# Second convolution of a residual block: two of six column positions also filtered along rows, norm sums of three images on ScalarE, and a map of two chunks between the convolutions

## The chip, the cores and the metric

The kernel runs on one core of a Trainium2 chip. The metric is the device time of one execution in microseconds; the page of the profile describes one profiled execution, and its "span" runs from that execution's first to its last instruction. The engines are named TensorE (PE; its weight loads are PEld), VectorE (DVE), ScalarE (ACT), GpSimd (POOL) and SyncE (SP). SP issues plain transfers, POOL issues those that add to their destination. A convolution of the code is written as matmuls in fp32, and each of them is two instructions in the trace.

## What is computed

Four layers on x of 4 images, 256 channels and 56 x 56 pixels. Every layer adds to x a function of its group norm. Layers 0 and 2 are involutions, layer 3 is a gating by means; only layer 1, a residual block of two 3 x 3 convolutions, is touched by the change:

```python
def _L1_conv_ref(x, w1, g1, b1, rm1, rv1, w2, g2, b2, rm2, rv2):
    h = _conv3x3(x, w1, stride=1)
    h = _bn(h, g1, b1, rm1, rv1)
    h = jax.nn.relu(h)
    h = _conv3x3(h, w2, stride=1)
    h = _bn(h, g2, b2, rm2, rv2)
    return jax.nn.relu(x + h)
...
def _gn(v, G=32, eps=1e-5):
    g = v.reshape(B_, G, C_ // G, H_, W_)
    m = jnp.mean(g, axis=(2, 3, 4), keepdims=True)
    s = jnp.var(g, axis=(2, 3, 4), keepdims=True)
    return ((g - m) / jnp.sqrt(s + eps)).reshape(v.shape)
...
x = x + _L1_conv_ref(_gn(x), L1_conv_w1, ...)
x = x + _L2_conv_ref(_gn(x), L2_conv_w1, ...)
```

The group norm of layer 2 needs a mean and a variance per channel of what layer 1 puts out.

## The kernel before

**Chunks.** An image goes through both convolutions in three chunks of rows: C1_ROWS (L56) for the first, C2_ROWS (L57: 16, 20 and 20 rows) for the second; with four images there are twelve chunks of each. The 256 channels are two halves (NB = 2) of 128 partitions. A list `order` alternates them: first convolution of chunk i, second convolution of chunk i - 1, and so on, with two chunks of the second convolution at the end.

**Columns.** Along a row, both convolutions work on transformed data: four output columns come from six products, the column positions k, with KS = (1, 2, 3, 4, 0, 5) as their order. `phases` (L1363, ScalarE at L1379) norms the loaded rows and spreads them into `ph1` by the column modulo 4; `transform` (L1382 to L1425, nine steps of VectorE) makes the six planes of a tile `v` from that. Two rows of each plane are kept from the chunk before (L1386).

**Rows.** The second convolution takes each position as it is: `unfiltered` (L1478 to L1484) sums six matmuls, three row taps times two input halves, for each output half, 12 per position, each over 14 columns times all rows of the chunk (280 columns at 20 rows, 224 at 16). The first convolution does better from its second chunk on: its positions are *filtered* along rows, two output rows from four products in place of six. `columns` (L1443) makes the inputs: an "inner" pair (sum and difference of two neighbouring rows, VectorE, L1464 and L1465) and an "outer" pair (difference of rows two apart: a multiplication by -1 on ScalarE, L1457, and a transfer from POOL that adds the other row, L1458). Then 16 matmuls of half the rows follow (L1520; 126 columns at 18 rows, 140 at 20). ScalarE copies the first product out of PSUM (L1529), VectorE forms difference and sum with the second (L1533, L1534) and adds the outer pair (L1536). The weights for this are formed once (`column_weights`, three VectorE instructions L1316 to L1318, and `filter_weights`, L1309).

**After the products.** In the second convolution VectorE and ScalarE join the positions (L1643 to L1666), position 0 and 5 by output half. `joined` then takes a half out: ScalarE scales it into a residual tile x (L1603), a transfer from POOL adds the input (L1604), ScalarE takes the relu (L1606), a second transfer adds the input again (L1607), and SP stores it (L1608). `late_r` puts the last three behind slots of the chunk that follows. In the chunk after that, VectorE takes the sums for the next norm from x with bn_stats (`stats`, L1633). The two last chunks take another way, with a residual tile `res` that both halves share (L1578, L1587, L1611, L1616).

**Order.** Every engine's order is that of the program (`in_order`). A chunk has twelve slots, `after[0]` to `after[11]`, two for each position, and the step loop (L1717 to L1801) drops other work into them: the transforms of the next chunks, the columns, the sums. So an instruction placed in a slot stands in its engine's queue between those of two positions.

**PSUM.** The stage has a pool of four tiles of two banks (L1187). An unfiltered position takes one, a filtered one two.

```python
            KS = (1, 2, 3, 4, 0, 5)

            def filtered(i):

                return KS[: (0, 5, 6)[min(i, 2)]]
...
                    place(after, late_v, (0, 0, 0, 1, 1))
...
                        place(after, input1(j), (1, 1, 2, 2, 3, 3, 4, 4, 5))
```

Of the kernel before, what the change touches and what calls it, by code (L numbers as in the profile page):

```python
# [16 lines left out]
P = 128  # L17
# [38 lines left out]
C1_ROWS = [(0, 20), (20, 38), (38, 56)]  # L56
# [16 lines left out]
def net_kernel(  # L73
# [1109 lines left out]
    def conv_layer(xin, xout, st, ahead):  # L1183
        with ExitStack() as es:
# [51 lines left out]
            v2_sb = wpool.tile([P, 2 * NY], F32, name="v2_sb")  # L1236

            def new_v2(half):

                n_v2[half] += 1  # L1240
                at = (n_v2[half] - 1) % 4
                if half:
                    return [room["v2"][:, at * NY : (at + 1) * NY]]
                if at == 3:
                    return [room[r][:, 5 * NY : 5 * NY + NY // 2] for r in ("v2", "xr")]
                t = room["v2"][:, 4 * NY : 5 * NY] if at == 2 else v2_sb[:, at * NY : (at + 1) * NY]
                return [t[:, : NY // 2], t[:, NY // 2 :]]
# [63 lines left out]
            def column_weights(ci, k0, k1):  # L1311

                w0, w1, w2 = (u1_sb[:, ci, y, k0:k1, :] for y in range(3))
                x = between_weights(ci, k0, k1)
                s = y_tile(5 if k0 == 5 else 3)[:, : (k1 - k0) * C].rearrange("p (k n) -> p k n", n=C)
                tt(s, w0, w2, ALU.add)  # L1316
                tt(x, s, w1, ALU.subtract)
                tt(w1, s, w1, ALU.add)  # L1318


            PL, VP = (0, 2, 1, 3), (0, 1, 2, 3, 5, 4)
            ph1 = wpool.tile([P, 4, CV_ROWS + 2, NB, WT + 1], F32, name="ph1")
            ph2 = wpool.tile([P, 4, H + 2, NB, WT + 1], F32, name="ph2")
# [3 lines left out]
            for j in range(4):  # L1327
                for y in (0, H + 1):
                    nc.gpsimd.memset(ph2[:, j, y], 0.0)
# [33 lines left out]
            def phases(i):  # L1363

                y0, y1, lo, hi = rows1(i)
                n, r0, known = y1 - y0 + 2, lo - (y0 - 1), 2 if i % 3 else 0
# [5 lines left out]
                for ci in range(NB):  # L1372
                    at = ci * (CV_ROWS + 2) * W
                    xr = room["rows"][:, at + known * W : at + (hi - lo) * W].rearrange("p (r t j) -> p j r t", t=WT, j=4)
                    for j in range(4):
                        q, t0 = (j + 1) % 4, (j + 1) // 4
                        dst = ph1[:, PL[q], r0 + known : r0 + hi - lo, ci, t0 : t0 + WT]
# [4 lines left out]
            def transform(v, ph, y0, n, known):  # L1382

                if known is not None:
                    old, m = known
                    nc.scalar.copy(  # L1386
                        v[:, :, : 2 * NB].rearrange("p k r t -> p k (r t)"),
                        old[:, :, m * NB : (m + 2) * NB].rearrange("p k r t -> p k (r t)"),
                    )
                    v, y0, n = v[:, :, 2 * NB :], y0 + 2, n - 2  # L1390
# [36 lines left out]
            v_sb = [wpool.tile([P, WPOS, (CV_ROWS + 2) * NB, WT], F32, name=f"v{k}") for k in range(2)]  # L1427

            def input1(i):
                y0, y1, _, _ = rows1(i)  # L1430
                v = v_of[1, i] = v_sb[min(i, 1)]
                p0, p1 = C1_ROWS[i % 3 - 1]
                known = (v_of[1, i - 1], p1 - p0) if i % 3 else None
                yield from transform(v, ph1, 0, y1 - y0 + 2, known)

            def input2(i):
                y0, y1 = C2_ROWS[i % 3]
                v = v_of[2, i] = v_sb[i == n_chunks - 1]
                p0, p1 = C2_ROWS[i % 3 - 1]
                known = (v_of[2, i - 1], p1 - p0) if i % 3 else None  # L1440
                yield from transform(v, ph2, y0, y1 - y0 + 2, known)

            def columns(i, k, half):  # L1443

                y0, y1, _, _ = rows1(i)
                n = y1 - y0
                m = n // 2
                v = v_of[1, i][:, VP[k]]
                if half:
                    (t,) = new_v2(1)  # L1450
                    v = v.rearrange("p r t -> p (r t)")
                    at = slice(0, n * NB * WT)
                    below = slice(2 * NB * WT, (n + 2) * NB * WT)
                    if i == 1:
                        tt(t[:, at], v[:, at], v[:, below], ALU.subtract)
                    else:
                        nc.scalar.mul(t[:, at], v[:, below], -1.0)  # L1457
                        nc.gpsimd.dma_start(t[:, at], v[:, at], accum_op=ALU.add)  # L1458
                    t = t.rearrange("p (r e n) -> p e r n", e=2, n=NB * WT)
                    v2_of[i, k, 1] = [t[:, e] for e in range(2)]  # L1460
                else:
                    v = v.rearrange("p (r e c) t -> p e r (c t)", e=2, c=NB)
                    t = v2_of[i, k, 0] = [x.rearrange("p (r n) -> p r n", n=NB * WT) for x in new_v2(0)]
                    tt(t[0][:, :m], v[:, 1, :m], v[:, 0, 1 : m + 1], ALU.add)  # L1464
                    tt(t[1][:, :m], v[:, 0, 1 : m + 1], v[:, 1, :m], ALU.subtract)  # L1465


            FIRST = [(k, half) for k in KS[:4] for half in range(2)]
# [16 lines left out]

            def conv1(i, after, tail):
# [3 lines left out]
                m = n // 2 * WT  # L1490
                a, t, b, s, q = (y_tile(k)[:, : NB * n * WT] for k in (0, 1, 2, 5, 4))
                first = s if i else q
                home = {1: s, 2: q, 3: t, 4: s, 0: y_tile(3)[:, : NB * n * WT], 5: s}

                def outputs(*js):
                    for j in js:
                        o = (a, t, b, q)[j].rearrange("p (c r t) -> p c r t", c=NB, t=WT)
                        p, t0 = PL[(j + 1) % 4], (j + 1) // 4
                        for co in range(NB):
                            nc.scalar.activation(  # L1500
                                ph2[:, p, y0 + 1 : y1 + 1, co, t0 : t0 + WT],
# [7 lines left out]
                for n_s, k in enumerate(KS):  # L1509
                    if k in filtered(i):  # L1510
                        va = v2_of[i, k, 0]
                        vb = v2_of[i, k, 1]
# [372 lines left out]
```

## Time and profile before

| what | us |
|---|---|
| median of 3 runs (range) | 1740.52 (1738.83 to 1744.15) |
| the profiled execution | 1735.74 |
| its span | 1733.9 |
| stage of the two convolutions | about 518 to 1186 |
| in that stage: PE, DVE, ACT, POOL busy | 662, 553, 295, 117 |

The stage's first matmul of a convolution starts at 517.87 us and its last ends at about 1186. Before and behind it are layer 0 and layers 2 and 3, in which the code is the same but for the place of their buffers. Busy time of an engine is the sum over its instructions; "idle before" is the time the engine waited, put down to what ended it. TensorE's clock was granted at 1.00 in every window of this stage that is shown.

### The profile page before, as it was taken

Reading aid. Unit: us, or ns where it says so; the run is one execution under the profiler, and the core shown is the slowest. Engines: PE = TensorE matmul, PEld = TensorE weight load, DVE = VectorE, ACT = ScalarE, POOL = GpSimd, SP = SyncE. Lnnn points to the kernel's source line nnn. Section 1 sums busy time; section 2 is a strip of 40 time slices with the busy share of each in tenths; the row PEclk is TensorE's granted clock in tenths of the full one; section 3 lists DMA queues with packets and bytes.
Section 4 is the critical chain, followed back from the end, with each engine's and each line's share of the span. In section 5 each row is a group of like instructions: output and inputs, shape, how many; then the busy total and the mean of one; then the engine's idle time right before and its main releaser. Section 6 shows DMA issues by size and latency. Waiting matters only on the chain.

```text
span 1733.9 us, 56359 instructions
## 1 busy us (share of the span) xinstructions
PE 1664.7 (96%) x24296; PEld 1479.3 (85%) x24296; DVE 1317.1 (76%) x2467; ACT 933.5 (54%) x2024; POOL 476.4 (27%) x669
## 2 busy tenths in 40 slices
PE   6999999999999999999999999998999899999998
PEld 4998998888977999898899889986988788788886
DVE  2777787777769887798878888856787678778775
ACT  2655556456646455443455245325667567577564
POOL 2223322323334111211122111100000563563571
PEclk9999999999989999999999999999999999999996
DMA  2455444543659546454565354553444666664652
GB/s 89 129 167 162 137 151 160 166 129 103 220 184 260 95 106 142 76 125 96 119 143 97 82 118 92 100 167 104 147 142 151 206 208 196 210 209 161 203 161 103
DMA packets 89030, 252.15 MB, mean 145 GB/s; under 512 B 14453, under 2 KB 35966, under 8 KB 85070
## 3 DMA queue, kind: packets, MB, share of 16 engines
q1 hardware_dynamic: 57438, 163.33, 29.1%
q0 software_dynamic: 30304, 83.95, 22.6%
q8 instruction: 192, 3.15, 0.8%
q10 hardware_dynamic: 1040, 1.26, 0.3%
q14 instruction: 56, 0.46, 0.1%
HBM read 95.07 MB, written 49.15 MB: 83 GB/s over the span
## 4 chain that ended last, share of the span: by engine, by line
PE 70%; DVE 15%; DMA 4%; ACT 4%; issue 3%; SPq 2%; POOL 2%; ACTq 0%; POOLq 0%; DVEq 0%
PE mm L1482 22%; PE ps L593 14%; PE ps L635 14%; PE mm L1520 11%; DVE kt L611 5%; PE ps L407 3%; DVE un L655 3%; DMA xw<-xw 2%; DMA u_sb<-in_wc_dram 2%; PE ps L469 2%; DVE st L1105 1%; ACT hp L488 1%; SPq L425 1%; ACT kt L604 1%; PE ps L718 1%
## 5 line engine op out<-in xcount | busy, mean ns | idle before, releaser
L1482 PE MATMUL mm<-v,u_sb 128*128 128x280 f32 (+2 forms) x1896 | 422.8, 384 | 0.7 <-DVE xs L1534 0.7
L1482 PEld LDWEIGHTS mm<-v,u_sb 128*128 128x128 f32 x1896 | 357.8, 189 | 62.2 <-issue 1.7
L635 PE MATMUL ps<-kt,xw 126*32 126x48 f32 (+1 forms) x12544 | 378.9, 235 | 20.9 <-issue 8.2
L635 PEld LDWEIGHTS ps<-kt,xw 126*32 126x32 f32 (+1 forms) x12544 | 340.6, 121 | 65.8 <-issue 41.5
L593 PE MATMUL ps<-hp,z_sb 64*126 64x133 f32 x6144 | 385.2, 279 | 9.2 <-DVE kt L611 5.0
L593 PEld LDWEIGHTS ps<-hp,z_sb 64*126 64x126 f32 x6144 | 365.1, 186 | 25.7 <-DVE kt L611 7.1
L611 DVE TENSOR_TENSOR kt<-ps,zb_sb 126x798 f32<-126x798 f32 x352 | 333.0, 980 | 59.4 <-PE ps L593 59.0
L604 ACT ACTIVATE kt<-ps,zb_sb 126x133 f32<-126x133 f32 x960 | 281.0, 442 | 108.4 <-PE ps L593 108.4
L655 DVE SCALAR_TENSOR_TENSOR un<-ps,s,un 128x240 f32<-128x240 f32 x224 | 102.4, 457 | 83.4 <-ACT un L650 79.3
L1520 PE MATMUL mm<-xs,u_sb 128*128 128x126 f32 (+1 forms) x1296 | 159.7, 277 | 4.4 <-DVE xs L1534 2.6
L655 DVE SCALAR_TENSOR_TENSOR un<-ps,par_sb,un 128x240 f32<-128x240 f32 x224 | 97.5, 456 | 82.0 <-ACT un L648 78.1
L1520 PEld LDWEIGHTS mm<-xs,u_sb 128*128 128x128 f32 x1296 | 153.3, 191 | 5.4 <-issue 2.9
L660 POOL TENSOR_TENSOR xs<-un,xs 128x240 f32<-128x240 f32 x112 | 72.1, 665 | 216.1 <-DVE un L655 216.1
L419 ACT COPY xw<-ps 126x896 f32<-126x896 f32 x112 | 101.4, 906 | 41.7 <-DMA xw<-xw 22.8
L1458 POOL DMA_DIRECT2D xs<-v x60 | 52.8, 1015 | 249.4 <-ACT xs L1457 248.5
L407 PE MATMUL ps<-ident_sb,strip_sb 128*126 128x128 f32 x784 | 111.6, 282 | 7.7 <-issue 4.3
L150 POOL TENSOR_TENSOR norm_sb<-norm_sb,mhalf 128x1 f32<-128x1 f32 x32 | 19.2, 601 | 360.5 <-DVE norm_sb L149 360.5
L648 ACT ACTIVATE un<-ps,par_sb 128x240 f32<-128x240 f32 x112 | 50.3, 449 | 119.4 <-PE ps L635 109.8
L650 ACT ACTIVATE un<-ps,bn_t,s 128x240 f32<-128x240 f32 x112 | 60.2, 538 | 88.2 <-PE ps L635 80.0
L407 PEld LDWEIGHTS ps<-ident_sb,strip_sb 128*126 128x126 f32 x784 | 84.2, 140 | 19.5 <-issue 5.4
L1603 ACT ACTIVATE xs<-hp,raw,raw 128x1120 f32<-128x1120 f32 (+1 forms) x20 | 45.2, 2260 | 97.7 <-DVE hp L1666 97.7
L1379 ACT ACTIVATE ph<-xs,norm_sb 128x294 f32<-128x294 f32 (+2 forms) x96 | 80.7, 865 | 9.5 <-DMA xs<-x 7.6
(291 smaller groups left out, 2010.0 us busy)
## 6 DMA issues: line engine op xcount, KB each, us to landing
xw<-xw SPq DMA_DIRECT2D x224, 252.0 KB
xw<-xw SPq DMA_DIRECT2D x224, 126.0 KB
xs<-x POOLq DMA_DIRECT2D x26, 560.0 KB, 5.9
x<-xs POOLq DMA_DIRECT2D x8, 1568.0 KB, 8.2
xs<-x SPq DMA_DIRECT2D x8, 1568.0 KB
xs<-v POOLq DMA_DIRECT2D x42, 252.0 KB, 4.2
xs<-in_x_dram SPq DMA_DIRECT2D x6, 1568.0 KB
x<-xs SPq DMA_DIRECT2D x6, 1568.0 KB
```

The source lines that it names most:

```text
L407: nc.tensor.transpose(ps[:Q, k * P : (k + 1) * P], flat[:, k * Q : (k + 1) * Q], ident_sb)
L419: nc.scalar.copy(xw[:, :NSB, :], ps[:Q, : NSB * P].rearrange("q (n c) -> q n c", n=NSB))
L593: nc.tensor.matmul(ps[:Q, i, k * NT : (k + 1) * NT], z_sb[i * R : (i + 1) * R, cb * GB // 2 + gp, z0 : z0 + Q], hp[i * R : (i + 1) * R, py ...
L604: nc.scalar.activation(kt[:, g0 + i, pb, :, k], ps[:Q, i, k * NT : (k + 1) * NT], AF.Identity, bias=zb_sb[:, cb * GB + g0 + i, p0 + k : p0 ...
L611: nc.vector.tensor_tensor(kt[:, g0 : g0 + 2, pb], ps[:Q, :, : PB * NT].rearrange("q i (k t) -> q i t k", k=PB), zb_sb[:, cb * GB + g0 : cb ...
L635: nc.tensor.matmul(v[m * j : m * j + m, i, :, k * TP : (k + 1) * TP], xw[:, window(ty), m * j : m * j + m], kt[:, ng * j : ng * j + ng, :, ...
L650: nc.scalar.activation(part, o[0], AF.Identity, bias=bn["t4"][:, cb : cb + 1], scale=bn["s4"][ng][:, 0, cb : cb + 1])
L655: nc.vector.scalar_tensor_tensor(part, o[e], s, part, ALU.mult, ALU.add)
L660: nc.gpsimd.tensor_tensor(dst, u, dst, ALU.add)
L1379: nc.scalar.activation(dst, xr[:, j], AF.Identity, bias=t, scale=s)
L1482: nc.tensor.matmul(ps, *position(u, v, ci, dy, k, co, n), start=(j == 0), stop=(j == NB * 3 - 1))
L1520: nc.tensor.matmul(ps[:, bank, co * m : (co + 1) * m], u[ci][:, co * P : (co + 1) * P], v2[e][:, : n // 2, ci * WT : (ci + 1) * WT], start ...
```

## The change

- *Two positions of the second convolution* (FILTERED2 = (4, 0)) are filtered along rows in every chunk, in the way of the first convolution. `filtered_product` is now shared. New weights (`column_weights2`, `filter_weights2`) are formed in the first chunk of the second convolution.
- *Inputs.* `inner_columns` takes two positions in one instruction; the pair (1, 2) goes into planes of `ph1` that are free then, so `phases` of the next chunk moves to later slots. `outer_columns` shares five buffers among both convolutions. The pair (0, 5) of the first convolution is made in its slot 0, its outer rows in slots 0 and 2.
- *Position 0* of the second convolution is now joined for both halves at once; position 5 stays by half. The two last chunks have a residual tile for each half.
- *Norm sums.* For images 0 to 2 bn_stats on VectorE goes. ScalarE runs over x twice with its accumulator: once for the mean, once, squared with the mean as bias, for the spread. Image 3 keeps bn_stats.
- *The way out.* The second half's first step (`leaves`) stands behind slot 0 of the next chunk; the store moves from slot 9 + 2 co to 11 + 2 co; the passes for the sums come at 10 + 2 co and 14 + 2 co (slots of 12 and more lie in the chunk after).
- *Rows and map.* C1_ROWS is 18, 20, 18, and `ph2`, which held a whole image between the convolutions, holds two chunks of 20 rows in turn, with an edge row set to zero where one is needed. The transform of the second convolution's chunk takes 19, 20 and 19 new rows (18, 20 and 20 before), and one of its steps moves from the second convolution's slot 0 to the first convolution's slot 10.

```diff
-C1_ROWS = [(0, 20), (20, 38), (38, 56)]
+C1_ROWS = [(0, 18), (18, 38), (38, 56)]
+PH_ROWS = 20
...
+            def new_inner(ks):
+                if ks == (1, 2):
+                    t = ph1[:, 1::2].rearrange("p k r c t -> p k (r c t)")[:, :, :NY]
+                else:
+                    n_v2[0] += 1
+                    t = v2_sb[:, n_v2[0] % 2]
...
+            FILTERED2 = (4, 0)
+            def column_weights2(ci, k):
+                s = y_tile(5)[:, :C]
+                column_sums_of(*(u2_sb[:, ci, y, k, :] for y in range(3)), ux2_sb[FILTERED2.index(k)][:, ci], s)
...
-            ph2 = wpool.tile([P, 4, H + 2, NB, WT + 1], F32, name="ph2")
+            ph2 = wpool.tile([P, 4, 2 * PH_ROWS, NB, WT + 1], F32, name="ph2")
...
+            def inner_columns(conv, i, *ks):
...
+                tt(t[:, :, 0, :m], v[:, :, 1, :m], v[:, :, 0, 1 : m + 1], ALU.add)
+                tt(t[:, :, 1, :m], v[:, :, 0, 1 : m + 1], v[:, :, 1, :m], ALU.subtract)
...
+            def outer_columns(conv, i, k):
...
+                if (conv, i) == (1, 1):
+                    tt(t[:, at], v[:, at], v[:, below], ALU.subtract)
+                else:
+                    nc.scalar.mul(t[:, at], v[:, below], -1.0)
+                    nc.gpsimd.dma_start(t[:, at], v[:, at], accum_op=ALU.add)
...
+            def filtered_product(conv, i, k, home, weights, between, items):
...
+                inner, outer = two_banks(), two_banks()
+                work4 = ((inner, 0, va[0], u1), (inner, 1, va[1], between), (outer, 0, vb[0], u0), (outer, 1, vb[1], u2))
+                for ps, bank, v2, u in work4:
+                    for co in range(NB):
+                        for ci in range(NB):
+                            nc.tensor.matmul(
+                                ps[:, bank, co * m : (co + 1) * m],
+                                u[ci][:, co * P : (co + 1) * P],
+                                v2[:, : n // 2, ci * WT : (ci + 1) * WT],
+                                start=(ci == 0),
+                                stop=(ci == NB - 1),
+                            )
...
+                nc.scalar.copy(o[:, 0], m1)
+                tt(o[:, 1], o[:, 0], m2, ALU.subtract)
+                tt(o[:, 0], o[:, 0], m2, ALU.add)
+                run_all(items)
+                tt(o, o, outer[:, :, : NB * m].rearrange("p e (r t) -> p e r t", t=WT), ALU.add)
...
+                        def leaves():
+                            nc.scalar.activation(x.rearrange("p (q j) -> p j q", j=4), y, AF.Identity, bias=t, scale=s)
+                            nc.gpsimd.dma_start(x, xin[bb][co][:, at], accum_op=ALU.add)
+                        if co == 0:
+                            leaves()
+                        else:
+                            late_r[0].append(leaves)
+                        k = 5 + 2 * co
                         late_r[k].append(lambda: nc.scalar.activation(x, x, AF.Relu, scale=by))
                         late_r[k + 1].append(lambda: nc.gpsimd.dma_start(x, xin[bb][co][:, at], accum_op=ALU.add))
-                        late_r[k + 4].append(lambda: nc.sync.dma_start(xout[bb][co][:, at], x))
+                        k = 10 + 2 * co
+                        late_r[k + 1].append(lambda: nc.sync.dma_start(xout[bb][co][:, at], x))
+                        if bb < B - 1:
+                            st = sums[co][:, i % 3]
+                            late_r[k].append(lambda: mean_of(st, x))
+                            late_r[k + 4].append(lambda: spread_of(st, x))
...
+                def mean_of(st, x):
+                    nc.gpsimd.memset(st[:, 0:1], float(n * W))
+                    nc.scalar.activation(x, x, AF.Identity, accum_out=st[:, 1:2])
+                    nc.scalar.mul(st[:, 1:2], st[:, 1:2], 1.0 / (n * W))
+                def spread_of(st, x):
+                    c = small.tile([P, 1], F32, name="c")
+                    nc.scalar.mul(c, st[:, 1:2], -1.0)
+                    nc.scalar.activation(x, x, AF.Square, bias=c, accum_out=st[:, 2:3])
...
-                for n_s, k in enumerate(KS[:4]):
+                for n_s, k in enumerate(KS[:5]):
+                    if n_s == 4:
+                        residual(0)
+                    if k in filtered2(i):
+                        ux = [ux2_sb[FILTERED2.index(k)][:, ci] for ci in range(NB)]
+                        filtered_product(2, i, k, s, u2_sb, ux, after[2 * n_s])
...
+                    else:
+                        stt(full(p), full(p), -0.75, got, ALU.mult, ALU.add)
+                        stt(p, r, 0.25, p, ALU.mult, ALU.add)
...
-                    ps = one_bank()[:, :m]
-                    unfiltered(ps, u2_sb, v, 0, co, n)
-                    stt(p[:, at], p[:, at], -0.75, ps, ALU.mult, ALU.add)
-                    stt(p[:, at], r[:, at], 0.25, p[:, at], ALU.mult, ALU.add)
...
-                tail += [[lambda co=co, k=k: stats(co, k) for k in range(ST_PIECES[i % 3])] for co in range(NB)]
+                if not summed or bb == B - 1:
+                    tail += [[lambda co=co, k=k: stats(co, k) for k in range(ST_PIECES[i % 3])] for co in range(NB)]
...
-                        place(after, late_v, (1, 3, 5, 8))
+                        place(after, late_v, (1, 3, 5, 8, 10))
...
-                            place(after, phases(i + 1), range(1, 10))
+                            place(after, phases(i + 1), range(4, 12))
...
-                        place(after, late_v, (0, 0, 0, 1, 1))
+                        place(after, late_v, (0, 0, 1, 1))
...
+                    if filtered2(i):
+                        after[2].append(lambda i=i: inner_columns(2, i, *filtered2(i)))
+                        for n, k in enumerate(filtered2(i)):
+                            after[2 + n].append(lambda i=i, k=k: outer_columns(2, i, k))
...
-                        for n, (k, half) in enumerate(FIRST):
-                            after[(5, 5, 6, 6, 7, 7, 8, 8)[n]].append(lambda j=j, k=k, half=half: columns(j, k, half))
+                        columns_at(after, (6, 8), ((4, 1), (4, 2), (6, 3), (9, 4)), 1, j)
```

## The prediction

> **What bounds the kernel now.** I read the page first: TensorE is busy nearly all the time, which alone says little. Columns: busy us, share of the span, instructions.
>
> ```profile
> span 1733.9 us, 56359 instructions
> PE 1664.7 (96%) x24296; PEld 1479.3 (85%) x24296; DVE 1317.1 (76%) x2467; ACT 933.5 (54%) x2024; POOL 476.4 (27%) x669
> ```
>
> Only the middle stage, about 518 to 1186 us, is touched, so the chain of waits there came second. Columns: start, us, what.
>
> ```profile
> 575.49 5.10 PE mm L1482 x24
> ...
> 663.45 22.88 PE mm L1520 x192
> ...
> 849.67 33.96 PE mm L1482 x144
> 883.63 21.44 PE mm L1520 x192
> 905.07 27.25 PE mm L1482 x144
> ```
>
> The reader is to see one engine without gaps: a second-convolution chunk (L1482) follows a first-convolution chunk (L1520) to the tenth of a microsecond. From 608 to 1183 us this chain is almost all TensorE, so here TensorE time removed is time won, unless another engine closes up. These rows price a matmul (each matmul of the code is two instructions in the trace): 33.96/144 = 235.8 ns at 280 columns, 27.25/144 = 189.2 at 224, 5.10/24 = 212.5 at 252, 22.88/192 = 119.2 at 140, 21.44/192 = 111.7 at 126.
>
> Third, windows by chunk, for what VectorE and ScalarE have left. Columns: window, length, then busy time of PE, PEld, DVE, ACT, POOL, the granted clock, DMA share and GB/s.
>
> ```profile
> 580.57:607.90 27.33, 27.33 (x148) 27.31 (x147) 24.30 (x43) 8.73 (x17) 4.61 (x6) 1.00 0.22 38
> 607.90:629.40 21.50, 21.50 (x194) 21.50 (x193) 17.79 (x36) 16.73 (x27) 5.09 (x6) 1.00 0.77 145
> 849.50:883.50 34.00, 34.00 (x147) 27.26 (x146) 27.88 (x51) 8.39 (x12) 4.40 (x5) 1.00 0.35 90
> 883.50:904.90 21.40, 21.40 (x193) 21.40 (x192) 17.54 (x35) 15.79 (x24) 4.36 (x5) 1.00 0.82 150
> 904.90:932.10 27.20, 27.20 (x146) 27.18 (x145) 25.32 (x45) 7.60 (x12) 3.53 (x4) 1.00 0.41 109
> 954.30:988.40 34.10, 34.09 (x146) 27.36 (x146) 28.63 (x49) 7.34 (x10) 4.37 (x5) 1.00 0.29 66
> ```
>
> VectorE is 82 to 93% busy, ScalarE under a third in the second convolution and three quarters in the first. VectorE is the engine that can close up. Its prices, from the groups of instructions by shape (count, then busy us and mean ns):
>
> ```profile
> L1633 DVE BATCH_NORM_STATS2 st<-xs 128x6 f32<-128x448 f32 x36 | 22.3, 619 | 0.0
> L1536 DVE TENSOR_TENSOR xs<-xs,mm 128x560 f32<-128x560 f32 x9 | 6.6, 737 | 2.3 <-PE mm L1520 1.7
> L1534 DVE TENSOR_TENSOR hp<-hp,mm 128x280 f32<-128x280 f32 x9 | 4.0, 447 | 0.3
> L1606 ACT ACTIVATE xs<-xs,norm_sb 128x1120 f32<-128x1120 f32 x12 | 14.7, 1224 | 0.0
> ```
>
> [...]
>
> **The change part by part.**
>
> *Filtered positions, 20-row chunks (8 of them).* Position by position, 24 instructions of 235.8 ns (5.66 us) become 32 of 140 columns, 119.2 ns (3.81). 1.85 x 2 positions x 8 chunks = -29.6 us, all on the path.
>
> *16-row chunks (4).* 24 x 189.2 = 4.54 us become 32 of 112 columns. No row shows 112. [...] the 126-column row a floor of 111.7. I take the floor[...]: 32 x 0.1117 = 3.57, saving 0.97 x 2 x 4 = -7.7 us. [...]
>
> *VectorE per 20-row chunk of the second convolution.* Added: inner sums of two positions, 2 x 0.74; the products' combination, 2 x (2 x 0.45 + 0.74) = 3.3. Removed: six bn_stats of the chunk before, 4 x 0.62 + 2 x 0.38 = 3.2 (after 16 rows: 4 x 0.62 = 2.5), for images 0 to 2. The first convolution's inner sums go from eight instructions to four of double length, -0.6; position 0 for both halves at once, -0.3; one transform step of about 1.2 moves to the first convolution. Net -0.5: 27.4 us in the window at 849.5, against 34.0 - 3.7 = 30.3 of TensorE. At 954 only four bn_stats go, so about 28.8. A 16-row chunk, whose window holds the bn_stats of the 20-row chunk ahead of it: 25.3 - 3.2 + 1.2 + 2.7 - 0.5 - 0.3 - 1.2 = 24.0 against 27.2 - 1.9 = 25.3. That is 90 to 95%. First convolution: 17.5 + 1.2 - 0.3 = 18.4 of 21.4. Per image VectorE has some 137 of 152 us. It fits, because TensorE may run ahead: four pairs of PSUM banks make it wait for VectorE only about two filtered positions (7 us) later, and a 16-row chunk's lag is recovered in the next first-convolution chunk, which has 3 us free. I cost this cover at nothing, with 2 us in all (0 to 8) for small waits.
>
> *Outer sums.* Each filtered position adds a ScalarE multiplication (0.67 at 560) and an accumulating transfer from POOL (0.87 to issue; 4.4 us to landing at L1458). Started at slots 2 and 3, about 7 to 8 us into the chunk, they land at 13 to 14; TensorE wants the first after three positions and half a filtered one, 3 x 4.54 + 1.8 = 15.4 (16 rows) or 18.9 (20 rows). Hidden; without that cover each late microsecond costs one per chunk.
>
> *Norm sums on ScalarE.* Per half two passes like L1606 (1.22 us at 1120) and two one-column multiplications. The accumulator is not in this trace: at the least it is free, at the most it is one more instruction[...]. I take 0.2. That is 4 x (1.22 + 0.2 + 0.28) = 6.8 us per chunk: 1.7 in the first convolution (16 to 17.7 of 21.4), the rest where ScalarE is idle. New waits: the first pass waits for the second accumulating transfer four slots earlier (7 us against 5.7 to land), the Square for the store that SP issues behind it. Queued behind the Square are the outer multiplications; POOL's transfers wait for those. SP's store comes ahead of load_rows, whose rows are read a whole chunk later. POOL gets one-column memsets and the edge rows, with 75% idle.
>
> *Second half of the residual's way out* (leaves, L1603, 2.4 us) goes behind the next chunk's first copy. Two stalls go where TensorE waits for L1534 behind that pass; in order of time (brackets: idle before, and who ended it):
>
> ```profile
> 829.98 1.19 PE L1520 MATMUL mm<-xs,u_sb 128*128 128x140 f32 x8 [0.54 <-DVE xs L1534]
> ...
> 993.30 1.19 PE L1520 MATMUL mm<-v_sb,u_sb 128*128 128x140 f32 x8 [0.53 <-DVE xs L1534]
> ```
>
> That is -1.1.
>
> *Rows 18/20/18.* Only image 0 differs: the unfiltered chunk saves 144 x (235.8 - 212.5) = 3.4 us, the next adds 160 x 7.5 ns + 24 x 23.3 ns = 1.8. But VectorE has hardly a gap from 526 to 580 us, and TensorE waits 4 us for it after 552; VectorE gains one inner sum and longer combinations there. I take +0.7 (-1.6 to +1.5).
>
> *New weights in the first second-convolution chunk.* Twelve instructions in VectorE's queue, 4 x 1.37 us (a triple at L1316 to L1318 takes that) = 5.5. VectorE in the first two windows: 24.3 + 17.8 + 5.5 + 1.2 + 2.5 - 0.3 - 0.6 - 0.3 = 50.1 against 27.3 - 1.9 + 21.4 = 46.8 of TensorE. It becomes the bound for 3.3 us, part of which the next chunk's slack repays: +2.5 (0 to 5).
>
> *Exit.* In the last chunk position 0 comes for both halves, so the first half's two long instructions (L1611, L1616, 3.6 us) push the second half's end from about 5.3 to 6.5 us after the last matmul, and the next layer's bias (L458) waits for it: +1.2 (-0.5 to +2). The map of two chunks (ph2) changes addresses and two memsets; no cost.
>
> Sum: -29.6 - 7.7 + 2 - 1.1 + 0.7 + 2.5 + 1.2 = -32.0 us. The span becomes 1701.9, the profiled execution 1735.7 - 32 = 1703.7. The median of the runs is 4.8 us above that execution; carried over, 1740.5 - 32 = 1708.5.
>
> **Rivals.** *Full saving*: VectorE's excess in image 0 is absorbed and 112 columns run below the floor. The steady gapless chain speaks for it, the busy VectorE against. -38 to -44: about 1699.
>
> *VectorE closes up*: at 90 to 95% every wait for a product shifts what follows, 1.5 us in each of eleven later chunks, 16.5 back: 1725. For it: VectorE waits for TensorE in the first convolution already. Against: the depth of PSUM.
>
> *Slower: ScalarE's queue blocks.* The Square waits for a store, the outer multiplications stand behind it, and TensorE waits for them at position 4. With w us late in eleven chunks the change loses from w = 2.9; at w = 5, -32 + 55 = +23: 1763. For it: the chain pass, store, Square, multiplication, transfer has only 2 us of slack in 16-row chunks. Against: SP is idle for most of a chunk, and 20-row chunks have 4 us more.
>
> **How the numbers follow.** Forecast (1703 to 1715) 0.56; full saving 0.16; VectorE closes up (1715 to 1735) 0.18; within 0.3% of before (5.2 us, what a measurement can tell) 0.03; slower 0.07. Faster is 0.56 + 0.16 + 0.18 = 0.90. The range 1698 to 1722 takes all of the first two and nearly half of the third.
>
> **What would show it.** Right: 20-row filtered products at 119 ns an instruction, two-position chunks of about 30.3 us, 16-row products at 111.7 ns, waits for VectorE only around 600 to 620 us. Wrong: idle time of TensorE at the filtered position released by the accumulating transfer or by ScalarE in every chunk; bn_stats' successors on ScalarE much over 1.4 us; a VectorE without gaps from 608 to 1150 us.

## The result and the profile after

| | before | after |
|---|---|---|
| median of 4 runs each, us (range of after) | 1739.84 | 1716.33 (1711.56 to 1720.71) |
| the profiled execution, us | 1735.74 | 1717.23 |
| its span, us | 1733.9 | 1715.5 |

The ratio of the times is 0.9859 (95% interval 0.9838 to 0.9880): the change saves 1.4%. The medians are 23.5 us apart, the two profiled executions 18.5; 32.0 were forecast. Of all the runs below one, the profiled run of the first experiment's kernel, fell into a slow state (1986 us, granted clock 0.747); its time and its trace are used nowhere. The page of the changed kernel opens so (busy us, share of the span, instructions):

```profile
span 1715.5 us, 57009 instructions
PE 1632.9 (95%) x24488; PEld 1466.1 (85%) x24488; DVE 1333.8 (78%) x2439; ACT 1000.9 (58%) x2192; POOL 498.2 (29%) x711
```

TensorE's busy time fell by 31.8 us, the span by 18.4 only: TensorE now stands idle for 13.4 us more. To find where, I compare the starts of the same chunks in the chains of waits of both kernels. This is the chain after (start, us, what), from the first 20-row chunk of the second convolution on:

```profile
635.58 16.98 PE mm L1525 x72
652.56 7.63 PE mm L1540 x64
660.19 5.66 PE mm L1525 x24
665.85 21.44 PE mm L1540 x192
...
740.43 13.62 PE mm L1525 x72
754.05 7.13 PE mm L1540 x64
761.18 4.56 PE mm L1525 x24
765.74 14.30 PE mm L1540 x128
```

Three unfiltered positions (L1525), then the two filtered ones (L1540, 64 instructions), one more unfiltered one, and the first convolution follows without a gap. A 20-row chunk takes 665.85 - 635.58 = 30.27 us (33.96 before), a 16-row chunk 765.74 - 740.43 = 25.31 (27.25 before). The filtered instructions take 7.63/64 = 119.2 ns at 140 columns and 7.13/64 = 111.4 at 112.

The same place in both kernels, in order of time:

| stretch | before, us | after, us | gained (-) or lost |
|---|---|---|---|
| start of the first 20-row chunk | 629.49 | 635.58 | +6.1 |
| from there to the start of the last chunk | 522.55 | 489.61 | -32.9 |
| the last chunk | 34.2 | 40.5 | +6.3 |
| its last matmul to the next layer's first product | 15.1 | 16.7 | +1.6 |
| from there to the end | 532.7 | 533.1 | +0.4 |

Sum -18.5. The middle holds the gain; the start and the last chunk, which repeats in no image, give a good third of it back. Of the 6.1 us at the start 1.7 lie ahead of the stage: VectorE's first transform (the first instruction of `transform`) starts at 513.16 us before and at 514.90 after, behind layer 0, whose code is the same. Windows of the changed kernel show the difference (window, length, busy PE, PEld, DVE, ACT, POOL, granted clock, DMA share, GB/s): the second chunk of the first convolution, the first of the second with the one behind it, two chunks of the middle, and the last.

```profile
550.30:584.00 33.70, 27.43 (x189) 25.71 (x187) 30.56 (x55) 19.03 (x36) 11.02 (x10) 0.95 0.93 154
584.00:635.60 51.60, 49.42 (x356) 48.62 (x355) 48.19 (x90) 30.75 (x62) 11.79 (x16) 0.97 0.48 86
840.50:870.77 30.27, 30.27 (x163) 25.77 (x162) 28.84 (x46) 13.72 (x27) 5.25 (x6) 1.00 0.55 132
893.65:918.96 25.31, 25.31 (x163) 25.29 (x162) 24.80 (x38) 13.11 (x26) 5.22 (x6) 1.00 0.61 148
1125.19:1165.74 40.55, 32.96 (x162) 27.94 (x161) 17.61 (x31) 13.39 (x11) 5.72 (x8) 0.92 0.45 111
```

In the middle TensorE is busy for the whole window although VectorE is at 95 and 98%. In the first and the last TensorE lacks 6.3 and 7.6 us, and in three of the five the granted clock is below 1. TensorE's own rows name who ended the waits (brackets: idle before, releaser):

```profile
557.41 1.22 PE L1540 MATMUL mm<-ph,u_sb 128*128 128x140 f32 x8 [2.94 <-DVE hp L1608]
565.07 1.45 PE L1540 MATMUL mm<-v_sb,u_sb 128*128 128x140 f32 x8 [3.00 <-DVE xs L1553]
612.28 1.13 PE L1540 MATMUL mm<-ph,u_sb 128*128 128x126 f32 x8 [1.92 <-DVE xs L1551]
1151.91 4.07 PE L1540 MATMUL mm<-u_sb 128*128 128x140 f32 x16 [7.59 <-DMA u_sb<-v]
```

The last row holds two things. TensorE waited 7.59 us for an accumulating transfer of an outer sum. And the 16 instructions behind it took 4.07 us where 16 x 119 ns = 1.9. Windows of 2 us behind that wait tell why (the clock is the third number from the end):

```profile
1150.00:1152.00 2.00, 0.09 (x1) 0.12 (x1) 0.00 (x0) 0.64 (x1) 0.54 (x2) 0.50 1.09 194
1152.00:1154.00 2.00, 2.00 (x9) 2.00 (x10) 0.00 (x0) 0.00 (x0) 0.00 (x0) 0.50 0.40 69
1154.00:1156.00 2.00, 2.00 (x10) 2.00 (x10) 0.00 (x0) 0.00 (x0) 0.00 (x0) 0.50 0.00 0
1156.00:1158.00 2.00, 2.00 (x16) 2.00 (x16) 1.91 (x3) 0.00 (x0) 0.00 (x0) 0.89 0.03 8
```

TensorE's granted clock is half for some 4 us. The last three windows lose 2 x (0.5 + 0.5 + 0.11) = 2.2 us. Windows at 566 to 570 (clock 0.50 and 0.67) and at 614 to 618 (0.50 and 0.72), behind the waits at 562 to 565 and 610 to 612, lose 1.7 and 1.6 in the same way: so much longer the matmuls took, which is the most that the half clock can have cost there.

Why was the transfer late? GpSimd's queue in the last chunk (start, us, what, idle before):

```profile
1133.34 0.88 POOL L1685 DMA_DIRECT2D xs<-x  x1 [28.17 <-ACT xs L1684]
1139.44 0.57 POOL L1686 DMA_DIRECT2D x<-xs  x1 [5.22 <-DMA xs<-x]
1140.04 0.86 POOL L1685 DMA_DIRECT2D xs<-x  x1
1147.13 0.55 POOL L1686 DMA_DIRECT2D x<-xs  x1 [6.23 <-DMA xs<-x]
1147.67 1.76 POOL L1508 DMA_DIRECT2D u_sb<-v  x2
```

The outer sums (L1508) stand behind the stores of the chunk before (L1686), and each store waits 5 to 6 us for the transfer in front of it to land. ScalarE's multiplications for L1508 were done at 1136.7, 11 us earlier. The head of this queue waits for ScalarE (L1684), which waited for a load, and SP shows that load's place (start, us, then the issue; SPq is SP's queue):

```profile
1104.51 15.18 SPq L296 DMA_DIRECT2D xs<-x  x2
1119.79 23.18 SPq L1392 DMA_DIRECT2D xs<-x  x2
```

The loads of the next layer's blocks (L296) could not leave for 15 us: they go to the buffer that holds outer sums of the second convolution, and SP waited 9.6 us for a transfer that fills it and 4.8 for a filtered product (L1540) that reads it; the last of these products ended at about 1119 us. The residual's second half (L1392) stood behind the loads. ScalarE had waited 9.43 us for it at 1128.49. Before, the second convolution had no outer sums in that buffer, and the same issue took 0.87 us.

### The profile page after: what moved, and what is told of

Its sections match the earlier page's. It is cut to its first block, busy times and chain, and to the rows that moved or that the text cites. A ratio compares the mean times of both kernels' runs of the same rounds, so it can differ in the third digit from the quotient of the medians.

```text
span 1715.5 us, 57009 instructions
## 1 busy us (share of the span) xinstructions
PE 1632.9 (95%) x24488; PEld 1466.1 (85%) x24488; DVE 1333.8 (78%) x2439; ACT 1000.9 (58%) x2192; POOL 498.2 (29%) x711
## 4 chain that ended last, share of the span: by engine, by line
PE 64%; DVE 15%; DMA 7%; issue 5%; ACT 3%; SPq 2%; POOL 2%; ACTq 0%; POOLq 0%; DVEq 0%
PE mm L1540 17%; PE ps L594 15%; PE ps L636 13%; PE mm L1525 11%; DVE kt L612 5%; DMA xw<-xw 4%; PE ps L408 3%; DVE un L656 3%; DMA u_sb<-in_wc_dram 2%; PE ps L470 1%; SPq L426 1%; SPq L427 1%; DVE st L1106 1%; ACT hp L489 1%; ACT xw L420 1%
## 5 line engine op out<-in xcount | busy, mean ns | idle before, releaser
L1525 PE MATMUL mm<-v,u_sb 128*128 128x280 f32 (+2 forms) x1320 | 295.1, 383 | 1.7 <-DVE xs L1551 1.0
L1525 PEld LDWEIGHTS mm<-v,u_sb 128*128 128x128 f32 x1320 | 247.5, 189 | 41.8 <-issue 1.6
L1540 PE MATMUL mm<-xs,u_sb 128*128 128x126 f32 (+2 forms) x1392 | 175.9, 279 | 0.3 <-DVE xs L1551 0.3
L1540 PEld LDWEIGHTS mm<-xs,u_sb 128*128 128x128 f32 x1392 | 168.5, 193 | 0.5 <-issue 0.5
L1508 POOL DMA_DIRECT2D xs<-v x82 | 75.2, 1006 | 285.3 <-ACT xs L1507 233.9
L1411 ACT ACTIVATE ph<-xs,norm_sb 128x266 f32<-128x266 f32 (+2 forms) x96 | 80.4, 862 | 9.0 <-DMA xs<-x 7.3
L1540 PE MATMUL mm<-v_sb,u_sb 128*128 128x140 f32 (+2 forms) x536 | 73.5, 280 | 3.5 <-DVE xs L1553 3.0
```

Of the source, the lines that this page charges most:

```text
L1411: nc.scalar.activation(dst, xr[:, j], AF.Identity, bias=t, scale=s)
L1525: nc.tensor.matmul(ps, *position(u, v, ci, dy, k, co, n), start=(j == 0), stop=(j == NB * 3 - 1))
L1540: nc.tensor.matmul(ps[:, bank, co * m : (co + 1) * m], u[ci][:, co * P : (co + 1) * P], v2[:, : n // 2, ci * WT : (ci + 1) * WT], start=(c ...
```

## The experiments

Times are given as the ratio to the kernel before with its interval; a difference of ratios times 1741 us (median of before beside these runs) gives us. The changed kernel stands at 0.9859.

**The last chunk, from GpSimd's side.** The outer sums are made by VectorE there, so neither ScalarE nor GpSimd takes part.

```diff
-                if (conv, i) == (1, 1):
+                if (conv, i) in ((1, 1), (2, n_chunks - 1)):
                     tt(t[:, at], v[:, at], v[:, below], ALU.subtract)
```

> In the last chunk of the second convolution the outer sums are made by VectorE (as those of its first chunk already are), so that neither ScalarE's multiplications nor GpSimd's transfers stand between the inner sums and TensorE there; all else as in the changed kernel. Theory (TensorE's 7.6 us wait in this chunk comes from GpSimd's queue, where the transfers stand behind the stores of the chunk before): the wait goes, and with it about 2.1 us of TensorE at half its granted clock behind it, while VectorE gets 2 to 3 us more work in the chunk; the chunk falls from 40.5 to about 31 to 33 us and the span by 7 to 10 us, to a time of about 1707 to 1710. Rival (the chunk is late because its inner sums or ScalarE's residual are late, and GpSimd's queue only shows it): TensorE still waits 5 us or more, for VectorE or ScalarE, and the time falls by less than 3.

Ratio 0.9813 (0.9782 to 0.9843), 8.0 us less. The theory named 7 to 10, the rival less than 3. The interval still touches that of the changed kernel, so the time alone is weak evidence. The chunk itself is read further down, in the run that holds the same edit together with another.

**The last chunk, from SP's side.** `ahead` loads the next layer's blocks (the text below calls them the first convolution's; there is no such work left).

```diff
                     if nxt == (2, n_chunks - 1):
-                        after[2].append(ahead)
+                        after[5].append(ahead)
```

> The block loads of the first convolution's next work are handed to SP after slot 5 of the last chunk but one, not after slot 2, so that the load of the residual's second half goes ahead of them in SP's queue. Theory (SP's queue starts the chain: residual load late, ScalarE's residual 9.4 us late, stores late, transfers of the outer sums behind them late): the residual's load is issued some 10 us or more earlier, the accumulating transfers of the chunk land earlier, TensorE's wait in the last chunk falls from 7.6 to 0 to 3 us, and the time falls by 5 to 9 us. Rival (the stores wait for something else, such as the accumulating transfers' own time): the wait stays within 2 us of 7.6 and the time within 2 us.

Ratio 0.9822 (0.9792 to 0.9852), 6.4 us less. The residual's load now comes first in SP's queue, and TensorE's wait shrinks. First SP's queue, then TensorE, of this kernel:

```profile
1103.13 7.69 SPq L1392 DMA_DIRECT2D xs<-x  x2
1110.91 7.82 SPq L296 DMA_DIRECT2D xs<-x  x2
```

```profile
1145.70 2.15 PE L1540 MATMUL mm<-u_sb 128*128 128x140 f32 x16 [2.33 <-DMA u_sb<-v]
```

Load 1119.79 to 1103.13, wait 7.59 to 2.33, and the 16 instructions in 2.15 us: no half clock. The last chunk takes 33.1 us in place of 40.5. The theory's numbers held (wait 0 to 3, time 5 to 9 less), though by the times alone this interval too overlaps that of the changed kernel. The chain is shown from both ends: SP's order starts it, GpSimd's order carries it to TensorE.

**The clock behind a wait.** 28 matmuls whose results are written over at once fill the wait in the last chunk; nothing else is changed.

```diff
                 for ps, bank, v2, u in work4:
+                    if (conv, i, k, ps is outer, bank) == (2, n_chunks - 1, FILTERED2[0], True, 0):
+                        for _ in range(28):
+                            nc.tensor.matmul(ps[:, 0, :m], u1[0][:, :P], va[0][:, : n // 2, :WT], start=True, stop=True)
```

> As the changed kernel, with 28 matmuls of 140 columns more (56 instructions of about 119 ns, 6.7 us), whose results are written over at once, just before TensorE's wait of 7.6 us in the last chunk. Theory (TensorE's granted clock is halved because TensorE has stood idle): the wait is filled but for about 1 us, the clock stays at 1.00 afterwards, and the 16 instructions behind the wait take 119 ns each rather than about 250: the last chunk gets 2 us shorter although more is computed. Rival (the clock falls for another reason, such as what came before, or the wait begins with the extra work): the clock is at 0.50 behind the wait as before, and the chunk is as long or longer. A time difference of 2 us is at the edge of what the runs tell; the trace decides.

TensorE's row at this place, and windows around it, in this kernel:

```profile
1152.57 2.17 PE L1543 MATMUL mm<-u_sb 128*128 128x140 f32 x16 [0.65 <-DMA u_sb<-v]
```

```profile
1152.00:1154.00 2.00, 1.43 (x12) 1.43 (x13) 0.00 (x0) 0.00 (x0) 0.00 (x0) 1.00 0.43 75
1154.00:1156.00 2.00, 2.00 (x19) 2.00 (x18) 1.19 (x2) 0.00 (x0) 0.00 (x0) 1.00 0.00 0
```

With TensorE kept busy the clock stays at 1.00 and the 16 instructions take 2.17 us in place of 4.07. The chunk is 38.1 us long in place of 40.5, with 6.7 us of work more in it. In four traces in which the same wait (6.5 to 7.6 us) isn't filled, the half clock follows each time. So here it came from the idle time. The times can't show 2 us: the ratio is 0.9878 (0.9854 to 0.9901), against 0.9838 to 0.9880 of the changed kernel. From the next layer's first product to the end, in code that is the same, this trace takes 541.8 us and that of the changed kernel 533.1.

**The start: the new weights.** GpSimd makes them beside the second chunk of the first convolution, in place of VectorE beside the first chunk of the second.

```diff
-                s = y_tile(5)[:, :C]
-                column_sums_of(*(u2_sb[:, ci, y, k, :] for y in range(3)), ux2_sb[FILTERED2.index(k)][:, ci], s)
+                w0, w1, w2 = (u2_sb[:, ci, y, k, :] for y in range(3))
+                gt = nc.gpsimd.tensor_tensor
+                s = room["xr"][:, NX : NX + C]
+                gt(s, w0, w2, ALU.add)
+                gt(ux2_sb[FILTERED2.index(k)][:, ci], s, w1, ALU.subtract)
+                gt(w1, s, w1, ALU.add)
...
                                 after[1].append(lambda ci=ci: filter_weights(ci, 0, 1))
+                                after[6 + 2 * ci].append(lambda ci=ci: column_weights2(ci, 4))
+                                after[11].append(lambda ci=ci: column_weights2(ci, 0))
...
-                                after[2 * n + ci].append(lambda ci=ci, k=k: column_weights2(ci, k))
```

> The filtered weights of the second convolution are made by GpSimd, beside the second chunk of the first convolution, not by VectorE beside the first chunk of the second: VectorE loses 12 instructions, about 5.5 us by their durations in the profile. Theory (the first chunk of the second convolution is 4.7 us longer than TensorE's own work because these stand in VectorE's queue): that stretch falls from 51.5 to about 47 us, the 1.9 us wait and the half clock behind it are gone, and the time falls by 4 to 5 us. Rival (VectorE is late there from the products and inner sums and from what it carries over of the chunk before): the stretch stays above 49.5 us and the time falls by less than 2, or rises if GpSimd delays what else stands in its queue.

The stretch goes from 582.4 to 630.1, 47.7 us in place of 51.5, and TensorE's wait in it from 1.92 to 0.43, without a half clock. The theory held, but the 3.8 us hold two things. In the run with the residual first and in that with the filled wait the new weights stand in VectorE's queue as in the changed kernel, and TensorE waits the same 1.92 us. Here are TensorE's wait and two windows behind it in the run with the residual first; the changed kernel has clocks of 0.50 and 0.72 in these windows:

```profile
612.96 1.13 PE L1540 MATMUL mm<-ph,u_sb 128*128 128x126 f32 x8 [1.92 <-DVE xs L1551]
614.00:616.00 2.00, 2.00 (x20) 2.00 (x20) 1.93 (x5) 0.00 (x0) 0.83 (x1) 1.00 0.34 62
616.00:618.00 2.00, 2.00 (x20) 2.00 (x20) 1.30 (x5) 1.33 (x1) 0.00 (x0) 1.00 0.41 75
```

The clock stays at 1.00, and the stretch takes 49.8 us in both of these runs. So the weights in VectorE's queue cost 2.1 us, and the half clock, which follows this wait in some executions only, 1.6 more. By the times alone (0.9831, 0.9804 to 0.9858, 4.9 us less) this edit is not told from the changed kernel; by the trace it is.

**The start: more of it.** The three instructions for position 0 of the first convolution go to GpSimd as well.

```diff
-            def column_sums_of(w0, w1, w2, x, s):
+            def column_sums_of(w0, w1, w2, x, s, tt=tt):
...
-                column_sums_of(*(u1_sb[:, ci, y, k0:k1, :] for y in range(3)), between_weights(ci, k0, k1), s)
+                ws = (u1_sb[:, ci, y, k0:k1, :] for y in range(3))
+                column_sums_of(*ws, between_weights(ci, k0, k1), s, tt if k0 else nc.gpsimd.tensor_tensor)
```

> As with the filtered weights of the second convolution on GpSimd, and besides those of position 0 of the first convolution too: VectorE loses six more instructions, 2.6 us, in the second chunk of the first convolution, where it has hardly a gap and TensorE waits twice for about 3 us. Theory (VectorE's queue is what makes this chunk 33.7 us against 24.7 of TensorE's own work): the chunk falls by 2 to 3 us more than with the other weights alone (which gave 32.0), to 29 to 30, and the time by another 2 to 3 us, to 1706 to 1710. Rival (the weights that arrive by DMA, or ScalarE's evacuations, set that chunk): it stays within 1 us of 32.0, and the time is 1711 to 1713.

A miss on both sides. The chunk became longer, 36.6 us (551.91 to 588.54), and the ratio is 0.9847 (0.9826 to 0.9868), 2.8 us more than with the second convolution's weights alone, a difference that the times can't tell from none. The chain of waits of this kernel tells why:

```profile
565.54 1.20 POOL u_sb L1320
566.81 0.73 POOL xs L1318
567.62 0.72 POOL xs L1319
568.43 0.73 POOL u_sb L1320
...
569.50 0.40 ACT xs L1314
...
570.21 0.29 ACT hp L1555
...
570.52 0.46 DVE hp L1556
...
571.60 3.50 PE mm L1546 x14
```

GpSimd needs until 569.16 for what VectorE had done by 564.4 in the changed kernel (of these 4.8 us, 2.1 are that the weights landed later, at 561.8 in place of 559.7). ScalarE's filter (L1314) waits for it, ScalarE's copy out of PSUM (L1555) stands behind the filter, VectorE waits for the copy (4.37 us) and TensorE for VectorE (3.84 us). An engine was relieved, and a wait put into the queue of another. It leaves open how much VectorE's load alone would give in this chunk.

**Norm sums back on VectorE.** One part of the change undone: bn_stats for images 0 to 2, in place of ScalarE's two passes.

```diff
-                        if bb < B - 1:
+                        if False:
...
-                if not summed or bb == B - 1:
+                if True:
...
-                            work.tile([P, 3, 3], F32, name="st3", bufs=4)
+                            new_sums(sum(ST_PIECES), work, 4)
```

> The second filtered position is kept, and the sums for the norm of the three images go back to VectorE's statistics instructions: one part of the change undone. VectorE has 8.9 us more per image, in stretches in which the profile of the changed kernel shows it busy for 95 to 98 per cent of the time in the second convolution's chunks and 80 per cent in the first's. Theory (VectorE has just enough room once the chunks are averaged over): the time rises by 0 to 8 us. Rival (VectorE is full with the filtered position, so that moving the sums is what pays for it): the time rises by 15 us or more, towards 3 x 8.9 = 27, and TensorE shows waits of 1 us and more for VectorE in most images.

Ratio 0.9929 (0.9904 to 0.9954), 12.2 us more: between theory and rival. From the first 20-row chunk to the start of the last it takes 1136.53 - 633.39 = 503.1 us, 13.5 more than the changed kernel. VectorE has 22.3 + 4.5 = 26.8 us more, so half is absorbed. Most of the rest comes out at one kind of place, the end of the first-convolution chunk that follows a 16-row chunk, ahead of the next 20-row one, for example:

```profile
788.60 6.61 PE L1525 MATMUL mm<-v,u_sb 128*128 128x280 f32 x21 [1.92 <-DVE xs L1551]
```

The same wait stands at 946.84 and 1104.13, and behind two of the three the clock falls (0.51 at 788 to 790, 0.50 at 1106 to 1108). TensorE's idle time at the three places is 6.8 us, and the half clock adds 3.6. The 16-row chunk has least room (24.80 of 25.31 us above); that it is its lag that surfaces there is read from the place, not tested. With the filtering, then, moving the norm sums is worth 12 us. That it would be worth nothing without the filtering fits the next run, but no run moves the sums alone.

**All but the filtering.** Every position of the second convolution is unfiltered, and all other parts are kept.

```diff
-            FILTERED2 = (4, 0)
+            FILTERED2 = ()
```

> All parts of the change stay but the filtered positions: every position of the second convolution is computed unfiltered again, so VectorE, ScalarE and GpSimd lose the work for inner and outer sums, combinations and weights there. Theory (the filtered positions carry nearly the whole gain, the other parts only make room for them): the time is that of the kernel before, less the 1.1 us of two stalls and 3 us either way for the first image's rows and the exit: 1735 to 1744. Rival (norm sums by ScalarE, the map between the convolutions and the pairs of inner sums gain something by themselves, or cost something that the filtering hides): below 1732 or above 1747.

Ratio 1.0009 (0.9997 to 1.0021): the theory's 1735 to 1744, no gain by themselves, taken together. The filtering, with the rest to carry it, is worth (1.0009 - 0.9859) x 1741 = 26 us. This run also shows the price of the first image's rows. The first chunk of the second convolution starts at 583.4 us, against 580.6 before; but VectorE's first transform starts 1.8 us later too, at 514.93 against 513.16, so the rows cost about 1.0 us here.

**Both repairs.** The edits of the first and the fourth experiment together.

> Two edits together: the last chunk's outer sums by VectorE and the filtered weights of the second convolution by GpSimd. Theory (two separate losses on TensorE's path, at its start and at its end): the gains add, 8 us and 5 us by the times of the two alone, so 1702 to 1706 and a ratio to the kernel before of about 0.977; the last chunk is 31 to 33 us long and TensorE's wait there is below 1 us. Rival (the earlier start only lengthens the wait at the end, or VectorE becomes late in the last chunk): 1708 or more, with TensorE waiting 3 us or more in the last chunk.

Ratio 0.9779 (0.9763 to 0.9794), 1702.24 us in the median, 13.9 us less than the changed kernel: 8.0 + 4.9 = 12.9, so they add. Its interval lies below that of the changed kernel. The two stretches at the start and the last chunk, as above, in this kernel:

```profile
551.63:584.08 32.45, 27.00 (x190) 25.45 (x188) 31.14 (x56) 17.48 (x34) 16.95 (x17) 0.95 1.00 166
584.08:631.50 47.42, 46.79 (x353) 46.45 (x352) 44.45 (x76) 30.41 (x59) 19.28 (x22) 1.00 0.50 94
1121.28:1151.70 30.42, 30.42 (x162) 25.67 (x161) 17.64 (x33) 11.09 (x9) 4.47 (x6) 1.00 0.48 130
```

The last chunk is 30.42 us, TensorE busy in all of it. VectorE has only 17.64 us there, and the outer sums cost it nothing that ends late. What is left at the start is the first row: VectorE at 31.14 of 32.45.

## Why the prediction came out as it did

**The direction and the mechanism were right, the size was too large by 8.5 us in the difference of the medians and by 13.5 us in the profiled executions.** That the median came near has some luck in it: 1716.3 us lies beyond the forecast's own 1703 to 1715, in the band named for "VectorE closes up", and what that rival says, 1.5 us lost in every later chunk, did not happen.

*Filtered positions, 20 and 16 rows.* Right. For the ten chunks of the middle the steps give 7 x 3.70 + 3 x 1.94 = 31.7 and two stalls of 0.54; measured 32.9. The 2 us held back for small waits weren't needed. In the rows of the kernel before, an instruction falls by 0.83 ns a column from 280 columns (235.8) to 140 (119.2); on that line 126 columns would be 107.6 ns, and their row has 111.7. That 112 columns would take as long was the author's estimate, and 111.4 came.

*VectorE per chunk.* Low by 0.4 to 1.4 us, which the cover took: 24.0 of 25.3 was forecast for 16 rows, 24.80 came; 27.4 for the chunk that starts at 840.50, 28.84 came; 28.8 for the one that starts at 940.97, 29.25 came. The 0.6 us for inner sums of double length are borne out: 444 ns at 280 elements (L1464, before) and 733 at 560 (L1491, after), so one in place of two saves 155. "VectorE closes up" did not happen in the middle, though with the norm sums put back it began to: that their move keeps VectorE below full is worth the 12 us of that run.

*Norm sums on ScalarE.* Right. The unknown accumulator was taken at 0.2 us; the groups of ScalarE's instructions by shape have it (count, busy us and mean ns):

```profile
L1698 ACT ACTIVATE xs<-xs,c 128x1120 f32<-128x1120 f32 x12 | 14.8, 1230 | 0.8 <-DMA x<-xs 0.4
L1698 ACT ACTIVATION_READ_ACCUMULATOR xs<-xs,c 128x1 f32 x18 | 3.4, 186 | 0.0
```

In the first pass it takes 193 ns (L1691). The one-column multiplications were taken at 0.28 us; they take 203 and 191 ns (L1692, L1697), and the one-column ScalarE instruction of the kernel before (L755) takes 271.

*Rows 18/20/18*, +0.7 (-1.6 to +1.5). Near: from VectorE's first transform to the second convolution's first chunk it takes 67.4 us before, 69.2 in the changed kernel and 68.4 without the filtering, so +1.8 and +1.0. VectorE's longer instructions (0.73 in place of 0.68 us each, without a gap there) belong to it; TensorE's waits there grow from 4.0 to 6.3 us.

*New weights in VectorE's queue*, +2.5 (0 to 5). Right. The forecast of 46.8 + 2.5 = 49.3 us for the stretch stands beside 49.8 in the two traces without a half clock there, and 47.7 with the weights elsewhere. The profiled execution of the changed kernel took 51.5; the difference is the half clock.

*Outer sums: "Hidden; without that cover each late microsecond costs one per chunk"*. **This is the step that failed, in one chunk of twelve.** It took one chunk's queue, alternating with the first convolution, for all of them. The last chunk follows another chunk of the second convolution directly, so its transfers stand on GpSimd behind two stores that wait for landings, and these behind loads that the new use of a buffer held up on SP. TensorE waited 7.6 us, and the chunk, from which the forecast took 3.7 us, became 6.3 us longer. The slower rival had this chain with ScalarE's queue as the place; it occurred with GpSimd's, once. In the other chunks TensorE waits for no transfer.

*Exit*, +1.2: measured +1.6.

*What no step had: TensorE's clock.* In the traces TensorE ran at half rate behind some of its waits, of 1.92 us and more: the granted clock was 0.50, and in the changed kernel's last chunk 16 instructions took 4.07 us, against 2.17 with that wait filled. This lasted 3 to 4 us in the changed kernel and up to 6.5 us elsewhere (at 558 to 564 us in the run without filtering, behind 3.13 us). So a wait of about 2 us or more carried, in these traces, a chance of a further loss: at most 1.7, 1.6 and 2.2 us at the three places in the profiled execution, 2.9 in the last chunk of the run with the second convolution's weights on GpSimd.

*The sum.* Stretch by stretch, forecast and trace lie apart by 10.0 us in the last chunk (7.6 of them the wait, 2.2 the clock behind it), 2.0 in the second convolution's first chunk with the one behind it (1.6 the clock), 1.1 in the rows ahead of it, 1.7 ahead of the stage, and 0.8 at the exit and behind it; the middle came out 2.1 better. That makes the 13.5 us.

## What to carry to other kernels

Cost a repeated chunk once for its steady form, and then go to the first and the last of them by name: what follows what in each engine's queue is different there, on SP and GpSimd above all. When a buffer gets a new reader, look at which issues wait for it, and at what stands behind those in the same queue. And where work is taken off a full engine, follow its results to the queue of the engine that waits for them.

## What the runs showed of the hardware

- In these traces the clock after a wait is not settled by the wait's length, nor by the code around it. Behind 7.6 us (the changed kernel), 7.5 (the norm sums on VectorE), 7.2 (the second convolution's weights on GpSimd), 6.5 and 3.8 (more weights there) it fell to 0.50 each time. Behind one and the same wait of 1.92 us in the first image it fell in two traces (the changed kernel at 612 us, the norm sums on VectorE at 610) and not in two others (the residual first at 613, the filled wait at 615). Behind the first wait of that image, at 557 to 562 us, it stayed at 1.00 after 2.94 us in the changed kernel and 3.04 in the run with more weights on GpSimd, and fell behind 2.9 in the runs with the residual first and the filled wait. The kernel before had waits of 2.1 and 1.2 us at 558 to 564 us with the clock at 1.00 throughout.
- GpSimd and VectorE took longer side by side at one place. In the run with more weights on GpSimd, a VectorE instruction of 560 elements took 2.15 us, where the others of its form take 0.73, while GpSimd began its first of 256 elements; and that took 1.12 us, where the last three of these six, with VectorE idle, take 0.72 to 0.73. By the spans shown the one that began first was slowed too. Not every such pair is slow: in the run with both repairs GpSimd's instructions of this form took 0.72 to 0.73 us from 572.09 to 574.4, with VectorE at work. No run isolates the cause.
